# A neighbour pick on TensorE: three 16-bit parts in one product of 192 columns, added by the identity afterwards

## The chip, the cores and the metric

The kernel runs on one core of a Trainium2 chip. The metric is device time in microseconds (us) of one launch without profiling, the median of three runs. One more execution is recorded by the hardware profiler; durations of single instructions come from that one.

## The reference, cut to what matters

There are 16 graphs (called entries here) of 1024 nodes with 64 features. Four layers follow each other, each with a residual and a layer norm: a small perceptron on summed messages (layer 0), a normalised adjacency product (layer 1), and two layers that take three weighted quantiles over each node's neighbours, per feature, after a dilation that takes some neighbours away, and then a perceptron (layers 2 and 3).

```python
vals = jnp.where(valid[..., None], x[:, None, :, :], big)
sv = jnp.sort(vals, axis=2)
...
for tau, wt in zip(TAUS, QWEIGHTS):
    pos = jnp.clip(tau * (mf - 1.0), 0.0)
    lo = jnp.floor(pos).astype(jnp.int32)
    hi = jnp.ceil(pos).astype(jnp.int32)
    frac = (pos - lo.astype(x.dtype))[..., None]
    q = gather(lo) * (1.0 - frac) + gather(hi) * frac
    agg = agg + wt * q
```

The two quantile layers are called table layers 0 and 1 below. All features are 32-bit.

## The kernel before, in words

**Stages of an entry.** `features` computes the first two layers and marks the neighbours. `lists` does the dilation, counts each node's neighbours, ranks the nodes by that count and builds a permutation matrix `order` (16-bit ones and zeros). Sorted by count, the nodes lie in eight tiles of 128; a tile is sorted at a fixed width (10 to 33 slots, SIZES), so few slots are empty. `ordered` permutes the features into that order and writes them to a table in memory.

**Two ways to fetch neighbours.** For the seven tiles with few neighbours, `lists` makes index lists and GpSimd gathers rows from the table (`gather`, L372 and L373, one indirect DMA a slot, 2944 of them). For the last tile, whose nodes have most neighbours, TensorE picks the rows (`fill`, from L778): for slot i (a level, 1 to 32) a one-hot matrix `hot` of 128 x 1024 is made from `place` (the rank of each node in each list), and `pick` (L365 to L370) multiplies its eight blocks with the features. To be exact, 32-bit features are split into three 16-bit parts that sum to them (`split`, L402); so a pick is 8 blocks x 3 parts = 24 products of 64 columns, all accumulated in one 64-column place of PSUM. There are 32 levels x 16 entries x 2 table layers = 1024 picks.

**Around the pick.** Of four levels, three have their `hot` made by VectorE (`is_equal`, in `fill`) and one by ScalarE (L808 and L809). Six `hot` buffers rotate (HOTS). Four levels share half a PSUM bank (`pgs`, two halves); when four are done, `empty` copies them with two ScalarE copies of 64 partitions x 256 columns (L800), one for each half of the rows, into the sort buffers. The copies of a group are placed when the next group's second level has been issued. For levels of 20 and more, one further product (L817) puts a large number where a node has no such neighbour.

**Permuting.** `ordered` multiplies `order` with three small columns (count, row, mask: `own`, L670), then with the three parts of the features (L369, tile `ordered_x`, 8 tiles x 24 products), copies the sum out (L691), sends it to the table on SyncE's queue (L692), and hands it to `parted`, which splits it anew into three parts for the fill of table layer 0 (`x0p`). `parted` does the same for layer 1 (`x1p`).

**Order of the work.** All engines run a written order. The work goes in 16 rounds; in a round two entries of one table layer are sorted on VectorE by exchange networks (`exchange`; its instructions have L212), and between the exchange operations `Weave` issues steps of the other generators (features, lists, ordered, fill, weigh, finish). Its clock is an estimate of VectorE's time; each `yield n` puts the next step n us later on it. A fill yields 2.4 for a level. An instruction that waits holds back what stands behind it on its engine.

**Names.** `pgk` is the PSUM bank of the picks; `got` the sort buffers of the last tile; `got_s` the gathered ones; `rest` the remainder in a split; `x2s` the permuted features; `pk` the products that give the lists (L632, L640); `pr`, `pa`, `there_o` other products, used here for their rates (L530, L476, L705). `L850` weighs sorted slots, `L651` makes the codes from which VectorE finds the lists.

```python
    def pick(dst, hot, parts, first=True):
...
        for c in range(NT):
            for q in range(3):
                nc.tensor.matmul(dst, hot[:, c, :], parts[:, c, q, :], start=first and c + q == 0,
                                 stop=c == NT - 1 and q == 2)
```

Of the kernel before, what the change touches and what calls it, by code (L numbers as in the profile page):

```python
# [12 lines left out]
F32 = mybir.dt.float32  # L13
F16 = mybir.dt.float16
BF = mybir.dt.bfloat16
# [7 lines left out]
P = 128  # L23
# [10 lines left out]
TABLES = 6  # L34
HOTS = 6
ROOM = 60
# [181 lines left out]
def adj_resnorm_kernel(ctx: ExitStack, tc: tile.TileContext, x, adj_t, nodemask, w01, b01, w02, b02,  # L218
# [28 lines left out]
    ONSET = HALF - P  # L247
    steps = const.tile([P, ONSET + N], BF, name="steps")
    row_id = const.tile([P, NT], F32, name="row_id")
    nc.gpsimd.iota(row_id, pattern=[[P, NT]], base=0, channel_multiplier=1,  # L250
# [113 lines left out]

    def pick(dst, hot, parts, first=True):  # L365

        for c in range(NT):
            for q in range(3):
                nc.tensor.matmul(dst, hot[:, c, :], parts[:, c, q, :], start=first and c + q == 0,  # L369
                                 stop=c == NT - 1 and q == 2)  # L370

# [45 lines left out]
    def features(b, e):  # L417
# [71 lines left out]
        yield from settle(x2, y, "x")  # L489
        while b and entries[b - 1].xs[0] is None:  # L490
            yield 2
        parts = s.feat.tile([P, NT, 3, C], BF, name="x2p", bufs=1)
        yield from split(x2, parts, y)
        e.x2p = parts

    def lists(b, e, pace):
# [67 lines left out]
        first_ones = steps[:1, ONSET : ONSET + P]  # L564
        own = s.work.tile([P, NT, 3], F16, name="own", bufs=1)
        key = s.work.tile([P, 5, NT], F32, name="key_c", bufs=1)
# [22 lines left out]

        dve.tensor_scalar(own[:, :, 0], key[:, 4], 1.0, None, op0=ALU.add)  # L590
        dve.tensor_copy(own[:, :, 1], row_id)
        dve.tensor_copy(own[:, :, 2], mask)
        dve.scalar_tensor_tensor(key[:, 0], own[:, :, 0], float(N), row_id, op0=ALU.mult, op1=ALU.add)
        keys = s.psum.tile([P, N], F32, name="keys", tag="big", bufs=2)
# [3 lines left out]
        for t in range(NT):  # L598
# [3 lines left out]
            yield 1.4  # L602
        yield 6
        dve.tensor_scalar(key[:, 2], key[:, 1], float(N - 1), 0.5, op0=ALU.add, op1=ALU.mult)
# [15 lines left out]
        nc.scalar.activation(minus_at, pn[:1], AF.Copy, scale=-1.0 / N)  # L620
        weave.add(ordered(b, e, order, own), 1.5, pace)

        e.idx = s.feat.tile([P, LINKS[-1]], I32, name="idx", bufs=6)
        pks, codes, found = {}, {}, []
        for t in (*reversed(range(NT)), -1, -2, -3):
# [19 lines left out]
            if 0 <= done < NT:  # L645
                if done == NT - 1:
                    e.there = s.work.tile([P, NT, P], BF, name="there", bufs=1)
                    nc.scalar.activation(e.there.rearrange("p c n -> p (c n)"), pks[done], AF.Sign)
                else:
                    codes[done] = s.work.tile([P, N], F16, name="code", tag="dist", bufs=3)  # L650
                    nc.scalar.activation(codes[done], pks[done], AF.Relu, scale=float(N))  # L651
# [12 lines left out]

    def ordered(b, e, order, own):

        ps = s.psum.tile([P, NT, 3], F32, name="ps", tag="s", bufs=1)
        for t in range(NT):
            for c in range(NT):
                nc.tensor.matmul(ps[:, t, :], order[:, c, t * P : (t + 1) * P], own[:, c, :],  # L670
                                 start=c == 0, stop=c == NT - 1)
        yield 9
        sorted_own = s.work.tile([P, NT, 3], F32, name="sorted_own", bufs=1)
        nc.scalar.copy(sorted_own, ps)
        count = sorted_own[:, :, 0]
        while e.x2p is None:
            yield 2
        px = s.psum.tile([P, NT, C], F32, name="ordered_x", tag="s", bufs=1)
        for t in range(NT):
            pick(px[:, t, :], order[:, :, t * P : (t + 1) * P], e.x2p)  # L680
            if t % 2:
                yield 2.5
        e.out_rows = s.feat.tile([P, NT], I32, name="out_rows", bufs=8)
        dve.tensor_scalar(e.out_rows, sorted_own[:, :, 1], float(b * N), None, op0=ALU.add)
        e.mask = s.feat.tile([P, NT], F32, name="mask_s", bufs=8)
        dve.tensor_copy(e.mask, sorted_own[:, :, 2])
        yield 7
        while b >= 4 and entries[b - 4].xs[1] is None:
# [3 lines left out]
        nc.sync.dma_start(table[0][b % TABLES][:N, :].rearrange("(t p) c -> p t c", p=P), e.xs[0])  # L692
        weave.add(parted(b, e, 0))
        while e.there is None:
            yield 2

        yield 4
# [80 lines left out]
    def fill(k):  # L778

        while k and (k - 1, NS - 1) not in free:  # L780
            yield 1
        middle, most = SIZES[NS - 2], SIZES[NS - 1]
        ends = [s.lists.tile([P, size, C], F32, name="got", tag=f"got_{size}", bufs=1) for size in (middle, most)]
        tails[k] = ends
        layer, both = members(k)
        groups = 0
        for low, high in ((1, middle), (middle, most)):
            for m, b, e in both:
                while e.parts[layer] is None or e.xs[layer] is None or e.place is None or e.none is None:
                    yield 1  # L790
                at = [(rows, ends[plan - LISTED], SIZES[plan]) for rows, plan in zip((lower, upper), halves_of(b))]
                if low == 1:
                    for rows, got, _ in at:
                        nc.scalar.copy(got[rows, 0, :], e.xs[layer][rows, NT - 1, :])
                waiting = None

                def empty():
                    for rows, got, size in at:
                        if waiting[0] < size:
                            nc.scalar.copy(got[rows, waiting[0] : waiting[0] + 4, :], waiting[1][rows])  # L800

                for i in range(low, high):
                    if i % 4 == 1:
                        first, pg = i, pgs[groups % 2]
                        groups += 1

                        by_act = s.lists.tile([P, NT, P], BF, name="hot", bufs=HOTS)
                        nc.scalar.activation(by_act, e.place, AF.Abs, bias=minus_k[:, i + 2 : i + 3])  # L808
                        nc.scalar.activation(by_act, by_act, AF.Relu, bias=one_f, scale=-1.0)  # L809
                    if i % 4 == 3:  # L810
                        hot = by_act
                    else:
                        hot = s.lists.tile([P, NT, P], BF, name="hot", bufs=HOTS)
                        dve.tensor_scalar(hot, e.place, float(i), None, op0=ALU.is_equal)
                    whole = i < LEAST[NS - 2]
                    if not whole:
                        nc.tensor.matmul(pg[:, i - first, :], e.none,  # L817
                                         ident_b[: KW - 1, i - 1 : i].to_broadcast([KW - 1, C]), start=True, stop=False)
                    pick(pg[:, i - first, :], hot, e.parts[layer], whole)
                    yield 2.4  # L820
                    if i % 4 == 2 and waiting:
                        empty()
                    if i % 4 == 0:
                        waiting = first, pg
                yield 5
                empty()
                yield 0.5
                if high == most:
                    e.filled[layer] = True
            filled.add((k, low))  # L830
# [38 lines left out]
    def finish(b, e, layer, agg, spare=False):  # L869
# [37 lines left out]
        if layer == 0:  # L907
            nc.sync.dma_start(table[1][b % TABLES][:N, :].rearrange("(t p) c -> p t c", p=P), xn)
            e.xs[1] = xn
            weave.add(parted(b, e, 1))  # L910
            return
# [6 lines left out]

    def parted(b, e, layer):

        back = 2 if layer else 3
        while splitting or (b >= back and not entries[b - back].filled[layer]):
            yield 2
        splitting.add(b)
        parts = s.feat.tile([P, NT, 3, C], BF, name=f"x{layer}p", bufs=back)
        rest = s.feat.tile([P, NT, C], F32, name="rest", bufs=1)
        yield from split(e.xs[layer], parts, rest)
        splitting.remove(b)
        e.parts[layer] = parts

    class Weave:
# [34 lines left out]
        def finish(self, gen):  # L966
            while self.runs(gen):
                self.advance()

    entries = [SimpleNamespace(near=None, taken=False, packed=False, listed=False, there=None, placed=False, x2p=None, place=None, none=None,  # L970
                               wts=None, parts=[None, None], xs=[None, None], filled=[False, False], ends=None) for _ in range(B)]
# [135 lines left out]
    with ExitStack() as main:  # L1107
# [9 lines left out]
        picked = s.psum.tile([P, 8, C], F32, name="pgk", bufs=1)  # L1117
        pgs = [picked[:, :4, :], picked[:, 4:, :]]
        ring = s.lists.tile([P, 2, ROOM, C], F32, name="got_s")
# [294 lines left out]
```

## Time and profile before

| what | value |
|---|---|
| median of 3 runs | 5103.43 us (5102.24 to 5104.99) |
| the profiled execution | 6960.85 us |
| its span, first to last instruction | 6959.1 us |
| instructions in it | 112,002 |
| mean granted TensorE clock | 0.690 |
| VectorE busy | 4338.6 us |
| ScalarE busy | 2838.3 us |
| GpSimd busy | 3219.1 us |
| TensorE products, busy as modelled | 4047.0 us, 44,824 products |

The profiled execution is much longer than the timed ones, so shares of its span can't be carried over as they are. PE stands for TensorE's products, PEld for its weight loads (beside the products), DVE for VectorE, ACT for ScalarE, POOL for GpSimd, SP for SyncE. A row of a group has: line, engine, operation, tiles and shapes, count, busy time and mean ns of one, and the idle time of the engine just ahead with what ended it. Ends of products are modelled, so the rate of products is read from a run of them, not from one. In a table of stretches each engine has its busy time in that stretch and the number of its instructions; PEclk is the granted clock, as a share of full.

### The profile page before, as it was taken

Reading aid. Unit: us, or ns where it says so; the run is one execution under the profiler, and the core shown is the slowest. Engines: PE = TensorE matmul, PEld = TensorE weight load, DVE = VectorE, ACT = ScalarE, POOL = GpSimd, SP = SyncE. Lnnn points to the kernel's source line nnn. Section 1 sums busy time; section 2 is a strip of 40 time slices with the busy share of each in tenths; the row PEclk is TensorE's granted clock in tenths of the full one; section 3 lists DMA queues with packets and bytes.
Section 4 is the critical chain, followed back from the end, with each engine's and each line's share of the span. In section 5 each row is a group of like instructions: output and inputs, shape, how many; then the busy total and the mean of one; then the engine's idle time right before and its main releaser. Section 6 shows DMA issues by size and latency. Waiting matters only on the chain.

```text
span 6959.1 us, 112002 instructions
## 1 busy us (share of the span) xinstructions
PE 4047.0 (58%) x44824; PEld 2895.5 (42%) x44824; DVE 4338.6 (62%) x9272; ACT 2838.3 (41%) x6388; POOL 3219.1 (46%) x3168
## 2 busy tenths in 40 slices
PE   6757657386557665666666566665756563333243
PEld 5435435254334443444445344443534443223232
DVE  2446537577647668485665858566574767557575
ACT  4336335354344445344433535334353443223232
POOL 0342225625453545454454644455453645665551
PEclk8778777597668766767676667766667675555555
DMA  3111102111111111111111111111111100000100
GB/s 87 46 44 50 49 24 49 40 48 42 46 31 40 43 43 35 36 45 32 43 41 41 37 34 44 32 43 40 43 34 27 34 18 22 21 21 17 22 19 6
DMA packets 416527, 255.23 MB, mean 37 GB/s; under 512 B 104554, under 2 KB 366842, under 8 KB 415994
## 3 DMA queue, kind: packets, MB, share of 16 engines
q1 hardware_dynamic: 317690, 147.12, 7.7%
q0 software_dynamic: 98304, 100.86, 6.8%
q8 instruction: 352, 5.77, 0.3%
q14 instruction: 181, 1.48, 0.1%
HBM read 235.18 MB, written 12.59 MB: 36 GB/s over the span
## 4 chain that ended last, share of the span: by engine, by line
PE 34%; DVE 28%; issue 20%; another core or an unknown queue 8%; ACT 7%; POOL 1%; DMA 1%; DVEq 0%; ACTq 0%; POOLq 0%
PE pgk L369 11%; DVE other L212 11%; DVE got_s L212 7%; PE pk L640 6%; DVE got L212 5%; PE pa L476 4%; PE px L445 2%; PE ordered_x L369 2%; PE pr L530 1%; ACT got_s L850 1%; PE pk L632 1%; POOL got_s L373 1%; DVE hot L212 1%; PE pk L638 1%
## 5 line engine op out<-in xcount | busy, mean ns | idle before, releaser
L373 POOL DMA_INDIRECT got_s<-table,idx x2944 | 3075.3, 1045 | 3514.5 <-issue 784.3
L369 PEld LDWEIGHTS <-hot 128*128 128x128 bf16 x24576 | 1092.7, 112 | 1821.9 <-issue 1488.7
L369 PE MATMUL pgk<-x0p,hot 128*128 128x64 bf16 x12288 | 655.0, 212 | 694.6 <-issue 517.1
L369 PE MATMUL pgk<-x1p,hot 128*128 128x64 bf16 x12288 | 664.4, 216 | 646.5 <-issue 407.4
L800 ACT COPY got<-pgk 64x256 f32<-64x256 f32 x416 | 151.9, 365 | 1976.7 <-PE pgk L369 1352.4
L212 DVE TENSOR_SCALAR hot<-place 128x1024 bf16<-128x1024 f16 x768 | 332.0, 435 | 730.2 <-remote 518.2
L640 PE MATMUL pk<-near,order 128*128 128x512 fp8e4 x1792 | 495.9, 419 | 56.2 <-issue 54.0
L212 DVE TENSOR_TENSOR other<-got_s 128x512 f32<-128x512 f32 (+9 forms) x850 | 507.7, 608 | 29.8 <-ACT got_s L1035 15.3
L212 DVE TENSOR_TENSOR got_s<-got_s 128x512 f32<-128x512 f32 (+9 forms) x867 | 483.6, 560 | 18.4
L530 PE MATMUL pr<-steps,near 128*128 128x512 bf16 x1536 | 420.2, 436 | 96.8 <-ACT junk L536 72.5
L476 PE MATMUL pa<-x,adj_r 128*128 128x65 f32 x2048 | 359.7, 332 | 165.7 <-issue 156.9
L850 ACT ACTIVATE got_s<-got_s,wts 128x64 f32<-128x64 f32 x1568 | 393.8, 335 | 79.6 <-DVE got_s L212 70.7
L476 PEld LDWEIGHTS pa<-x,adj_r 128*128 128x128 f32 x2048 | 344.1, 251 | 177.5 <-issue 166.9
L212 DVE TENSOR_TENSOR got_s<-other 128x512 f32<-128x512 f32 (+9 forms) x731 | 401.2, 562 | 9.5 <-DVE other L212 1.5
L212 DVE TENSOR_TENSOR other<-other 128x384 f32<-128x384 f32 (+10 forms) x617 | 322.3, 522 | 17.1
L651 ACT ACTIVATE code<-pk 128x1024 f16<-128x1024 f32 x112 | 114.2, 1020 | 511.7 <-PE pk L640 344.5
L212 DVE MAX8 best<-code 128x8 f16<-128x1024 f16 x240 | 293.8, 1224 | 45.3 <-ACT code L651 32.3
L445 PE MATMUL px<-adj_r,x_s 128*64 128x128 f32 x2048 | 291.6, 299 | 47.4 <-issue 35.0
L640 PEld LDWEIGHTS <-order 128*128 128x128 bf16 x1792 | 167.3, 103 | 327.2 <-issue 197.4
L536 ACT ACTIVATE junk<-pr,nb_st 128x1024 f16<-128x1024 f32 x256 | 281.6, 1106 | 52.0 <-remote 21.8
L530 PEld LDWEIGHTS <-near 128*128 128x128 fp8e4 x1536 | 165.6, 110 | 327.9 <-issue 199.4
L809 ACT ACTIVATE hot<-hot,one_f 128x1024 bf16<-128x1024 bf16 x256 | 293.9, 1148 | 12.7 <-remote 4.4
(215 smaller groups left out, 7095.5 us busy)
## 6 DMA issues: line engine op xcount, KB each, us to landing
adj_r<-in_adj_dram SPq DMA_DIRECT2D x256, 512.0 KB
got_s<-table,idx POOLq DMA_INDIRECT x2944
x_s<-in_x_dram SPq DMA_DIRECT2D x16, 256.0 KB
table<-x2s SPq DMA_DIRECT2D x16, 256.0 KB
table<-x3s SPq DMA_DIRECT2D x16, 256.0 KB
out_dram<-agg,out_rows POOLq DMA_INDIRECT x128
table<-no_row SPq DMA_DIRECT2D x12, 0.2 KB
w01s<-in_L_gnn_W_dram SPq DMA_DIRECT2D x1, 32.0 KB
```

The source lines that it names most:

```text
L212: return call(*args, **kwargs)
L369: nc.tensor.matmul(dst, hot[:, c, :], parts[:, c, q, :], start=first and c + q == 0, stop=c == NT - 1 and q == 2)
L373: nc.gpsimd.indirect_dma_start(out=dst, out_offset=None, in_=tab, in_offset=bass.IndirectOffsetOnAxis(ap=rows, axis=0))
L445: nc.tensor.matmul(px[C:, q * P : (q + 1) * P], x_s[:, jt, :], adj[t][:, jt, :], start=jt == 0, stop=jt == NT - 1)
L476: nc.tensor.matmul(pa[:, q, :], adj[i][:, jt, :], x1[:, jt, :], start=jt == 0, stop=jt == NT - 1)
L530: nc.tensor.matmul(pr[:, h * HALF : (h + 1) * HALF], near[:, c, t * P : (t + 1) * P], steps[:, ONSET + h * HALF - c * P :][:, :HALF], star ...
L536: nc.scalar.activation(junk, prs[t - 1], AF.Sign, bias=lim[:, i, t - 1 : t], scale=-1.0, accum_out=cut_at[:, i, t - 1 : t])
L640: nc.tensor.matmul(cols, order[:, c, rows], left(c, slice(h * G, (h + 1) * G)), start=False, stop=c == NT - 1)
L651: nc.scalar.activation(codes[done], pks[done], AF.Relu, scale=float(N))
L800: nc.scalar.copy(got[rows, waiting[0] : waiting[0] + 4, :], waiting[1][rows])
L809: nc.scalar.activation(by_act, by_act, AF.Relu, bias=one_f, scale=-1.0)
L850: nc.scalar.activation(got[:, m, i, :], got[:, m, slot_id, :], AF.Copy, scale=e.wts[:, t, i : i + 1])
```

## The change

A pick becomes eight products of 192 columns: the three parts lie side by side, and the sum over the eight blocks is made for each part apart. ScalarE then copies the three sums (128 x 192, 32-bit in PSUM) to a 16-bit tile `brought`, and three products with the identity add them in PSUM. Each sum has one term that isn't zero, so the 16-bit copy loses nothing. Two places of 192 columns (`sides`), two of 64 (`pgs`) and two `brought` tiles rotate; all of PSUM's places are in the bank that `pgk` had. Copies into the sort buffers are made for two levels at a time, 64 x 128. The level's add is issued two levels after its pick, ScalarE's copy half a step before that add.

`ordered` works likewise: the split features and four small columns (count, two parts of the row number, mask) lie side by side in `moved` (196 columns), are permuted together in eight products a tile, two tiles at a time, and the copied parts serve the fill of table layer 0 as they are; three identity products of 512 columns give the 32-bit features. The second split for table layer 0 goes. Six `hot` buffers become five, and `there` becomes an 8-bit tile.

```diff
-HOTS = 6
+HOTS = 5
+OWN = 4
...
-    def pick(dst, hot, parts, first=True):
+    def pick(dst, hot, parts):
 
         for c in range(NT):
-            for q in range(3):
-                nc.tensor.matmul(dst, hot[:, c, :], parts[:, c, q, :], start=first and c + q == 0,
-                                 stop=c == NT - 1 and q == 2)
+            nc.tensor.matmul(dst, hot[:, c, :], parts[:, c, :, :], start=c == 0, stop=c == NT - 1)
+
+    def add_up(dst, parts, first=True):
+
+        for q in range(3):
+            nc.tensor.matmul(dst, ident_b, parts[:, q, :], start=first and q == 0, stop=q == 2)
...
-        yield 6
+        yield 9
...
+        while e.moved is None:
+            yield 1
+        moved = e.moved
+        dve.tensor_scalar(moved[:, :, 0], key[:, 4], 1.0, None, op0=ALU.add)
+        dve.tensor_copy(moved[:, :, 1:3], row_parts)
+        dve.tensor_copy(moved[:, :, 3], mask)
...
-                    e.there = s.work.tile([P, NT, P], BF, name="there", bufs=1)
+                    e.there = s.work.tile([P, NT, P], F8, name="there", bufs=1)
...
+        while not e.split or (b >= 3 and not entries[b - 3].filled[0]):
+            yield 1
+        sorted_own = s.work.tile([P, NT, OWN], F32, name="sorted_own", bufs=1)
+        parts = s.feat.tile([P, NT, 3, C], BF, name="x0p", bufs=3)
         count = sorted_own[:, :, 0]
-        while e.x2p is None:
-            yield 2
+        for g in range(0, NT, 2):
+            po = s.psum.tile([P, 2, OWN + 3 * C], F32, name="moved_o", tag="s", bufs=1)
+            for t in range(g, g + 2):
+                for c in range(NT):
+                    nc.tensor.matmul(po[:, t - g, :], order[:, c, t * P : (t + 1) * P], e.moved[:, c, :], start=c == 0,
+                                     stop=c == NT - 1)
+            yield 3.6
+            nc.scalar.copy(parts[:, g : g + 2], po[:, :, OWN:].rearrange("p t (q c) -> p t q c", c=C))
+            nc.scalar.copy(sorted_own[:, g : g + 2, :], po[:, :, :OWN])
+            yield 1.2
         px = s.psum.tile([P, NT, C], F32, name="ordered_x", tag="s", bufs=1)
-        for t in range(NT):
-            pick(px[:, t, :], order[:, :, t * P : (t + 1) * P], e.x2p)
-            if t % 2:
-                yield 2.5
+        for q in range(3):
+            nc.tensor.matmul(px, ident_b, parts[:, :, q, :], start=q == 0, stop=q == 2)
+        e.parts[0] = parts
...
-        weave.add(parted(b, e, 0))
...
-                    pick(pg[:, i - first, :], hot, e.parts[layer], whole)
-                    yield 2.4
-                    if i % 4 == 2 and waiting:
-                        empty()
-                    if i % 4 == 0:
-                        waiting = first, pg
...
+                for i in range(low, high + 3):
+                    if low <= i - 2 < high:
+                        at_i, sb = i - 2, brought[i % 2]
+                        whole = at_i < LEAST[NS - 2]
+                        pg = pgs[:, (at_i - low) % 2, :]
...
+                        add_up(pg, sb, whole)
+                    if i < high:
...
+                        pick(sides[i % 2], hot, e.parts[layer])
+                    yield 1.2
+                    if low <= i - 1 < high:
+                        nc.scalar.copy(brought[(i - 1) % 2], sides[(i - 1) % 2])
+                    if low <= i - 2 < high and (i - 2 - low) % 2:
+                        for rows, got, size in at:
+                            if i - 3 < size:
+                                nc.scalar.copy(got[rows, i - 3 : i - 1, :], pgs[rows])
+                    yield 1.2
...
-        pgs = [picked[:, :4, :], picked[:, 4:, :]]
+        sides = [picked[:, 3 * i : 3 * i + 3, :] for i in range(2)]
+        pgs = picked[:, 6:, :]
+        brought = [s.lists.tile([P, 3, C], BF, name=f"brought{i}") for i in range(2)]
```

The instruction lists of the two programs differ by: 24,576 weight loads of `hot` become 8192 and 6912 of `order` become 3840; 3120 products with the identity come in; on ScalarE 1024 copies of 128 x 192 and 832 of 64 x 128 come in, and 416 of 64 x 256 go. VectorE has 10,562 entries in both: 32 operations of 512 columns give way to small ones.

## The prediction

> **What bounds the kernel now.** I read the page first: engine totals, then the chain of work that ended last.
>
> ```profile
> PE 4047.0 (58%) x44824; PEld 2895.5 (42%) x44824; DVE 4338.6 (62%) x9272; ACT 2838.3 (41%) x6388; POOL 3219.1 (46%) x3168
> ...
> PE 34%; DVE 28%; issue 20%; another core or an unknown queue 8%; ACT 7%; POOL 1%; DMA 1%; DVEq 0%; ACTq 0%; POOLq 0%
> PE pgk L369 11%; DVE other L212 11%; DVE got_s L212 7%; PE pk L640 6%; DVE got L212 5%; PE pa L476 4%; PE px L445 2%; PE ordered_x L369 2%; PE pr L530 1%; ACT got_s L850 1%; PE pk L632 1%; POOL got_s L373 1%; DVE hot L212 1%; PE pk L638 1%
> ```
>
> It looks as if TensorE (PE) and its picks (L369) lead. But the profiled execution took 6960.85 us (span 6959.1, 1.75 around it) and the median is 5103.43: 1857 us are in the profiled execution only, or nearly. The chain says which: "issue" 19.5% and "unknown" 7.8% of 6959 are 1357 + 543 = 1900 us. The timeline shows what such a stretch is:
>
> ```profile
> 208.33 1.90 PE L476 MATMUL pa<-x,adj_r 128*128 128x65 f32 x16
> ...
> 242.52 0.29 PEld L476 LDWEIGHTS pa<-x,adj_r 128*128 128x128 f32 x1 [2.51 <-issue]
> 243.92 0.27 PE L476 MATMUL pa<-x,adj_r 128*128 128x65 f32 x1 [2.53 <-issue]
> 245.32 0.29 PEld L476 LDWEIGHTS pa<-x,adj_r 128*128 128x128 f32 x1 [2.51 <-issue]
> 246.72 0.27 PE L476 MATMUL pa<-x,adj_r 128*128 128x65 f32 x1 [2.53 <-issue]
> ```
>
> Sixteen products take 1.90 us; 35 us later one PE instruction starts every 1.40 us and waits for nothing shown. I take this as the price of recording 89,648 PE instructions, and look at stretches of 50 us in which issue and unknown are small:
>
> ```profile
> core 0: us, PE busy (x) PEld busy (x) DVE busy (x) ACT busy (x) POOL busy (x), PEclk, DMA share, GB/s
> 1400.00:1450.00 50.00, 49.17 (x639) 35.50 (x636) 44.77 (x78) 25.21 (x50) 0.00 (x0) 1.00 0.24 66
> 2150.00:2200.00 50.00, 42.94 (x615) 32.37 (x614) 47.42 (x110) 24.60 (x66) 15.17 (x16) 0.93 0.24 64
> 4300.00:4350.00 50.00, 30.35 (x334) 24.38 (x335) 48.30 (x94) 28.24 (x55) 24.82 (x23) 0.77 0.17 46
> 2600.00:2650.00 50.00, 29.60 (x155) 14.19 (x156) 47.81 (x114) 37.15 (x102) 22.88 (x22) 0.77 0.12 24
> 3450.00:3500.00 50.00, 20.16 (x133) 12.21 (x131) 48.51 (x102) 33.39 (x79) 34.80 (x30) 0.63 0.09 21
> ```
>
> The first three hold picks, the last two none. VectorE (DVE) is busy 44.8 to 48.5 of 50 us in all. And 4338.6 us of its work in 5103 is 85%; only 765 us are idle, much of it start and end. So the timed run is bound by DVE, and by PE only where picks meet other PE work (the first row).
>
> **What a pick costs.** The rate of PE is read from bursts on the chain:
>
> ```profile
> 313.90 0.70 PE pgk L369 x24
> ...
> 325.79 1.40 PE pgk L369 x48
> 327.19 2.59 PE pr L530 x12
> ```
>
> A load and a product of 64 columns: 0.70/24 = 29 ns. One of 512: 2.59/12 = 216. The 128-column products of L705 (32 in 1.79 us) take 56. That is 0.42 ns a column, with nothing for the weight load. The Trainium skill, "TensorE: Matmul & The Clock Gate", section "Back-to-back issue gap", gives N/2.4 + 2.5 ns and a floor near 25 ns: 29, 56 and 216, as here (its sustained 81 and 131 ns for 128 and 512 columns are not what this trace has). So 192 columns take an estimated 82 ns. The same page, section "Weight-path perf modes — Fast Weight Load (FWL) and DoubleRow", says a 16-bit load of 128 columns is sped up several times; the 29 ns agree. Loads are therefore no cost that sharing them could save.
>
> **The change part by part.** All against the profiled execution's rows; I carry the sum to the median, since the 1857 us between them are not in it.
>
> 1. *Picks* (32 levels x 16 entries x 2 layers = 1024). Removed: 24 pairs x 29 = 0.70 us. Added: 8 x 82 = 0.66 and three adds of 64 columns, 0.09: 0.75 us. +0.05 x 1024 = +51 us of PE at full clock, in proportion at half clock. PE ends a third of the chain: +17. Bounds: 0 (all beside DVE) and +51.
>
> 2. *ScalarE (ACT) copies.* Its rows:
>
> ```profile
> L800 ACT COPY got<-pgk 64x256 f32<-64x256 f32 x416 | 151.9, 365 | 1976.7 <-PE pgk L369 1352.4 <-remote 524.2 <-issue 37.2
> L452 ACT COPY node_in<-px 64x512 f32<-64x512 f32 x32 | 18.6, 580 | 50.9 <-remote 21.8 <-issue 16.1 <-PE px L445 12.6
> ```
>
> 0.84 ns a column, so 192 columns 0.31 us and 128 columns 0.26. Added: 1024 x 0.31 + 832 x 0.26 = 534; removed: 416 x 0.365 = 152. +382 us. ACT's "ScalarE: Activation LUTs", section "What ACT_TABLE_LOAD costs", has 186 ns + 0.833 a column, 346 for 192: same slope, 30 ns above these rows. Not shown before: a copy of 192 to bf16; I take 0.31 (bounds 0.23, overlapped, and 0.35). ACT ends 7% of the chain with 41% busy, 17% of its work: 382 x 0.17 = +65. Bounds: 0, since ACT was idle 2265 us of 5103, and +150, where each late copy holds up what is queued behind it (weighing L850, code L651), for which DVE waits.
>
> 3. *Ordering* (16 times). Removed: 192 x 29 + 64 x 25 = 7.2 us of PE; added 64 x 84 (196 columns) + 3 x 216 = 6.0. -19 in all; a third: -6. ACT: 64 copies of 384 (0.47) and 64 of 8 (0.15) for 48 casts of 0.6 and 16 small copies: +8, nothing on the path. The table's write on SP's queue and POOL's gathers behind it now follow four rounds of products and copies through one bank, some 4 x 0.6 us of ACT later; from the third pair on this lies beside the round before, for the first entries it is exposed: +2, in the rounding. The 8-bit "there" (L648), the two iotas and the list's new wait for the split rows cost nothing that I can name: the same products and copies, and rows that are split a layer earlier than they are used.
>
> 4. *The second split of layer 0 goes.*
>
> ```profile
> L212 DVE TENSOR_TENSOR rest<-x2s,x0p 128x512 f32<-128x512 f32 x16 | 11.0, 688 | 49.5 <-ACT x0p L405 34.2 <-issue 15.3
> L212 DVE TENSOR_TENSOR rest<-rest,x0p 128x512 f32<-128x512 f32 x16 | 11.0, 687 | 40.1 <-issue 31.7 <-ACT x0p L409 8.2
> ```
>
> -22 us of DVE; 32 small operations (about 0.17 each) come in: +5. Before them DVE sat 90 us; 47 are "issue". Of 42 for ACT I take 20. Sum -37; bounds -107 and -17.
>
> 5. *Slack.* Hot tiles 6 to 5, and the pick's room from eight levels to two: PE's add waits for ACT's copy of a level issued only half a step before, and queued behind that add are the later picks and all else in PE's order. Who waits: DVE, at the next hot tile, its queue with it.
>
> ```profile
> DVE hot L212 <- PE pgk L369: 200.7, 49, 19.9
> ```
>
> In the first clean stretch that wait was 4.0 of 50 us, in the other two none. Fills take some 170 of each round's 290 us, 2700 us in all; a third more of a wait of at most 8% is +70, at least 0. I take +20. New small wait: ordering holds for a layer-0 fill three entries back; it comes a round before the gathers need it, so nothing.
>
> Sum: +17 + 65 - 6 - 37 + 20 = +59. Made against the profiled execution without its stalls: 6960.85 - 1900 = 5061, within 1% of the median. Forecast 5103 + 59 = 5162, say **5160**.
>
> **Rivals.** (a) *ACT in lockstep with PE*: copies at 1024 places where ACT waits for the pick just issued, against 208. For: L800 alone waited 1977 us. Against: ACT has 2265 - 390 = 1875 us free. It decides when a level's wait passes 1875/1024 = 1.8 us; at 2.0 us ACT is the bound: 2838 + 390 + 2048 = 5276. (b) *Fewer instructions help the timed run too; faster.* DVE's work at 95% busy is 4339/0.95 = 4567; start idle is some 200 us (233 in the first 350). 336 us of 5103 stay unexplained. If they are PE stalls of the kind in the timeline and go with PE's instructions (89,648 to 56,976, -36%), that is -121: 5162 - 121 = 5041, and 4945 where parts 2 and 5 are hidden as well. Against: 1900 us of stall match the whole excess of the profiled execution. It decides from 59/0.36 = 164 us of such stalls on. (c) *Nothing moves*: copies are hidden, slack is enough, part 4 is eaten: 5103 within 0.2%.
>
> **Numbers.** Forecast (slower, 5115 to 5230) 0.44; (a) 0.11; (b) 0.34, most of it from 4945 to 5090; (c) 0.11. Two in ten outside: low 4960 (nearly all of (b)), high 5290 (just past (a)'s). A difference below 0.2% can't be told from none here. Slower 0.55, same 0.11, faster 0.34.
>
> **What would show it.** Pick: 8 products in about 0.7 us on the chain, PE's busy time for them not smaller per level. ACT busy up by 300 to 400 us; DVE down by some 17. The profiled span should fall far more than the median: stalls 1900 x 0.64 = 1208, so about 6370, with 80,840 instructions. Lockstep would show as ACT's "brought" copies waiting for picks over 1.8 us each. I am wrong if clean stretches show DVE busy no less, yet the median falls over 100 us: then the stalls were in the timed run; or if products of 192 columns take clearly less than 82 ns.

## Result, and the profile after

The changed kernel takes 5480.36 us (median of 4 runs, 5478.82 to 5482.86); the kernel before 5103.78 beside it. The ratio is 1.0738, with a 95% interval of 1.072 to 1.0757: slower by 377 us, not by the 57 forecast, and above the range. Several chips were used: on some the kernel before has medians of 5103 to 5105 us, on others of 6986 to 7001, so every ratio below is within one chip. Differences in us between runs of the first kind can be across its chips, which agree within 2 us in the medians of the kernel before. Both medians here are of the first kind; the profile of before, with its 6960 us and 27% of its chain spent waiting for nothing shown, was probably taken on the second (the record doesn't name its chip).

The page of the changed kernel, engine totals and chain:

```profile
span 5478.8 us, 81153 instructions
PE 3723.2 (68%) x28385; PEld 2701.2 (49%) x28488; DVE 4330.0 (79%) x9272; ACT 3181.8 (58%) x7898; POOL 3319.1 (61%) x3170
...
PE 35%; DVE 33%; ACT 20%; issue 4%; POOL 3%; DMA 3%; ACTq 0%; DVEq 0%; POOLq 0%
```

The span is that of the other runs, and "issue" is 4% of the chain instead of 20%. DVE has about the same work as before (4330 against 4338.6) but is idle 1149 us. For a comparison of idle time the profile of before is of no use, being so much longer; the nearest on the first kind of chip is the kernel with the new ordering and the old picks (e15 below):

```profile
span 5068.0 us, 106032 instructions
PE 3474.6 (69%) x41800; PEld 2592.5 (51%) x41800; DVE 4314.6 (85%) x9272; ACT 2842.5 (56%) x6452; POOL 3338.3 (66%) x3170
```

There DVE is idle 753 us. The spans differ by 411 us, and 395 of these are idle DVE. Busy time per 500 us shows that the loss is found in all three stretches looked at, not in one place. First the changed kernel, then e15:

```profile
1000.00:1500.00 500.00, 348.51 (x2673) 250.78 (x2685) 415.78 (x875) 293.74 (x716) 301.55 (x282) 0.79 0.24 56
2000.00:2500.00 500.00, 354.73 (x2742) 256.15 (x2751) 439.37 (x935) 319.40 (x814) 340.38 (x313) 0.77 0.22 49
3000.00:3500.00 500.00, 345.36 (x2621) 251.51 (x2633) 440.81 (x954) 323.06 (x795) 332.66 (x306) 0.76 0.22 50
```

```profile
1000.00:1500.00 500.00, 373.60 (x4450) 274.95 (x4450) 457.35 (x942) 313.89 (x699) 339.60 (x313) 0.83 0.25 59
2000.00:2500.00 500.00, 393.27 (x4944) 295.48 (x4941) 462.62 (x982) 305.59 (x708) 379.39 (x349) 0.83 0.25 59
3000.00:3500.00 500.00, 361.71 (x4420) 269.23 (x4420) 468.35 (x1001) 313.33 (x706) 360.82 (x329) 0.83 0.24 57
```

The columns after the window's length are busy PE, PEld, DVE, ACT and POOL. DVE does 416 to 441 us of work in a window instead of 457 to 468. PE and POOL do less than there too, and ACT about the same (936 us in the three windows, against 933). So no other engine has become full; they wait for one another.

The groups that answer to L800 and to the split's remainder:

```profile
L831 ACT CAST brought<-pgk 128x192 bf16<-128x192 f32 x1024 | 323.5, 316 | 1201.8 <-PE pgk L373 1157.5 <-PE pgk L378 38.9 <-issue 0.5
L378 PE MATMUL pgk<-brought,ident_b 128*128 128x64 bf16 x3072 | 296.1, 212 | 429.6 <-ACT brought L831 245.2 <-ACT got L835 184.2
L835 ACT COPY got<-pgk 64x128 f32<-64x128 f32 x832 | 216.1, 260 | 45.4 <-PE pgk L378 40.2
```

```profile
L213 DVE TENSOR_TENSOR rest<-x3s,x1p x16: 683/685/693, 932.8 to 5127.9; 128x512 f32<-128x512 f32 x16
```

Sizes are as forecast: 0.316 us a copy (0.31), 0.26 a sum's copy, and only layer 1 is still split in `parted`. What the forecast didn't have: ACT sat 1158 us ahead of the copies, waiting for picks, and PE 429 us ahead of the additions, waiting for ACT. DVE's wait at the hot tiles:

```profile
DVE hot L213 <- PE pgk L373: 274.7, 95, 9.9
```

(total, times, longest). It was 50.6 in e15, which has six hot tiles. In e3 below, with five of them and the old fill, it was 115.5, so a part of the rise may belong to the missing tile. Added up by cause over DVE's waits, PE went from 179 to 443 us, ACT from 241 to 406, DMA from 151 to 116: +394, the difference in idle time (395) but for rounding.

The timeline shows how it goes, here 12 us of a fill of layer 1:

```profile
2010.16 0.82 PE L373 MATMUL pgk<-x1p,hot 128*128 128x192 bf16 x8
...
2011.02 0.32 ACT L831 CAST brought<-pgk 128x192 bf16<-128x192 f32 x1 [1.06 <-PE pgk L373]
...
2011.39 0.25 PE L378 MATMUL pgk<-brought,ident_b 128*128 128x64 bf16 x3 [0.41 <-ACT brought L831]
...
2013.38 1.15 ACT L821 ACTIVATE hot<-place,minus_k 128x1024 bf16<-128x1024 f16 x1
...
2013.49 0.82 PE L373 MATMUL pgk<-x1p,hot 128*128 128x192 bf16 x8
...
2014.56 1.15 ACT L822 ACTIVATE hot<-hot,one_f 128x1024 bf16<-128x1024 bf16 x1
...
2015.74 0.32 ACT L831 CAST brought<-pgk 128x192 bf16<-128x192 f32 x1
...
2016.11 0.25 PE L378 MATMUL pgk<-brought,ident_b 128*128 128x64 bf16 x3 [1.79 <-ACT brought L831]
...
2021.03 1.47 PE L373 MATMUL pgk<-x1p,hot 128*128 128x192 bf16 x8
...
2022.53 0.32 ACT L831 CAST brought<-pgk 128x192 bf16<-128x192 f32 x1 [1.69 <-PE pgk L373]
```

By the code, the copy behind pick i takes the side of pick i - 1, which was done long before. Yet at 2011.02 and 2022.53 it starts 0.04 and 0.03 us after the *newest* pick ends (2010.98, 2022.50), with ACT idle for over a microsecond ahead of it. So the two sides are no two buffers: the copy waits for the last product into `pgk`, whatever its place. The built program says the same: 1020 of the 1024 copies wait for the newest product into `pgk` that was issued ahead of them (for the other four, ACT had made that wait before), and where an addition waits for a copy out of `pgk`, it is the newest one. And the next addition waits for that copy, if need be behind two 1.15 us activations for a hot tile, which stand ahead of it on ACT (1.79 us). Each level sends PE to ACT and back.

### The profile page after: what moved, and what is told of

The parts are those of the page before. It is cut to its first block, busy times and chain, and to the rows that moved or that the text cites. A ratio compares the mean times of both kernels' runs of the same rounds, so it can differ in the third digit from the quotient of the medians.

```text
span 5478.8 us, 81153 instructions
## 1 busy us (share of the span) xinstructions
PE 3723.2 (68%) x28385; PEld 2701.2 (49%) x28488; DVE 4330.0 (79%) x9272; ACT 3181.8 (58%) x7898; POOL 3319.1 (61%) x3170
## 4 chain that ended last, share of the span: by engine, by line
PE 35%; DVE 33%; ACT 20%; issue 4%; POOL 3%; DMA 3%; ACTq 0%; DVEq 0%; POOLq 0%
DVE other L213 12%; PE pgk L373 9%; DVE got_s L213 8%; PE pk L651 6%; DVE got L213 6%; PE pa L484 4%; ACT brought L831 3%; ACT hot L822 2%; ACT got_s L859 2%; PE px L453 2%; DMA got_s<-table,idx 2%; ACT hot L821 2%; POOL got_s L381 2%; PE pgk L378 2%; ACT got L835 2%
## 5 line engine op out<-in xcount | busy, mean ns | idle before, releaser
L381 POOL DMA_INDIRECT got_s<-table,idx x2944 | 3175.6, 1079 | 1966.7 <-issue 631.7
L831 ACT CAST brought<-pgk 128x192 bf16<-128x192 f32 x1024 | 323.5, 316 | 1201.8 <-PE pgk L373 1157.5
L373 PEld LDWEIGHTS <-hot 128*128 128x128 bf16 x8192 | 851.5, 119 | 325.7 <-DVE hot L213 278.9
L373 PE MATMUL pgk<-x1p,hot 128*128 128x192 bf16 x4096 | 587.0, 306 | 221.2 <-DVE hot L213 205.4
L378 PEld LDWEIGHTS <-ident_b 128*128 128x128 bf16 x3072 | 214.5, 108 | 826.7 <-issue 798.7
L378 PE MATMUL pgk<-brought,ident_b 128*128 128x64 bf16 x3072 | 296.1, 212 | 429.6 <-ACT brought L831 245.2
L373 PE MATMUL pgk<-x0p,hot 128*128 128x192 bf16 x4096 | 551.0, 293 | 48.7 <-DVE hot L213 42.2
L213 DVE TENSOR_TENSOR got_s<-got_s 128x128 f32<-128x128 f32 (+10 forms) x867 | 484.1, 562 | 44.1 <-ACT got_s L859 26.0
L651 PE MATMUL pk<-near,order 128*128 128x512 fp8e4 x1792 | 434.9, 387 | 0.0
L821 ACT ACTIVATE hot<-place,minus_k 128x1024 bf16<-128x1024 f16 x256 | 293.3, 1146 | 7.3 <-DVE place L213 3.7
```

What stands on the lines that cost most here:

```text
L213: return call(*args, **kwargs)
L373: nc.tensor.matmul(dst, hot[:, c, :], parts[:, c, :, :], start=c == 0, stop=c == NT - 1)
L378: nc.tensor.matmul(dst, ident_b, parts[:, q, :], start=first and q == 0, stop=q == 2)
L381: nc.gpsimd.indirect_dma_start(out=dst, out_offset=None, in_=tab, in_offset=bass.IndirectOffsetOnAxis(ap=rows, axis=0))
L651: nc.tensor.matmul(cols, order[:, c, rows], left(c, slice(h * G, (h + 1) * G)), start=False, stop=c == NT - 1)
L831: nc.scalar.copy(brought[(i - 1) % 2], sides[(i - 1) % 2])
```

## Experiments

Theory (lockstep): what costs is each place in ACT's order at which it must stop for the newest pick, and PE's stop for ACT after it. First rival: ScalarE's added work. Second: the wider products and additions on TensorE, or the fifth hot tile gone.

**The parts alone.** e1 takes the changed kernel's ordering, and the picks, six hot tiles and copies by fours of before; e2 the opposite; e3 is the kernel before with `HOTS = 5`; e4 the changed kernel without the copies.

```diff
 # e1, against the changed kernel
-HOTS = 5
+HOTS = 6
...
-                        pick(sides[i % 2], hot, e.parts[layer])
+                    pick(pg[:, i - first, :], hot, e.parts[layer], whole)
...
 # e2, against the kernel before: the other way round
 # e3, against the kernel before
-HOTS = 6
+HOTS = 5
 # e4, against the changed kernel
-                    if low <= i - 1 < high:
-                        nc.scalar.copy(brought[(i - 1) % 2], sides[(i - 1) % 2])
...
+        for still in brought:
+            nc.vector.memset(still, 1.0)
```

> The new ordering (features and small columns permuted side by side, no second split for table layer 0) with the picks, the six hot tiles and the group copies of before. If the loss comes from the hand-over of each pick between TensorE and ScalarE (lockstep), this is at or a little below the kernel before: 5040 to 5110 us. If it comes from the ordering, whose wait for an earlier fill makes the gathers late, it is 5250 us or more. By the forecast's part 4 alone it gains some 40 us.

> The new picks with five hot tiles, the ordering and its second split as before. Lockstep: most of the loss stays, 5420 to 5560 us. If the ordering is to blame, under 5300 us.

> The kernel before with five hot tiles in place of six, nothing else. Lockstep: a small cost, 5105 to 5150 us. If the missing hot tile makes VectorE wait for TensorE, 5250 us or more.

> The changed kernel without ScalarE's copies of the three sums (the adds take a constant tile, so the picked features are left out of the last tile's values). 1024 copies of 0.316 us and both hand-overs of each are gone. Lockstep, or ScalarE's added work: 5000 to 5200 us. If the ordering, the hot tiles or the products themselves are to blame: over 5380 us.

Beside 5105.1 us of before: e1 5066.93 (ratio 0.9924, 0.9907 to 0.994), e2 5565.94 (1.0897, 1.0878 to 1.0915), e3 5112.04 (1.0012, 1.0005 to 1.0019), e4 5179.02 (1.0133, 1.0109 to 1.0157). The ordering gains 38 us, the fill loses 5480 - 5067 = 413 on top of it, and leaving out the copies gives 301 of these back. With the old ordering the fill loses 461 (e2; 6 us above the range expected, the other three lie in theirs). A hot tile less costs 7 us in the kernel before; in the changed kernel, a sixth one was not tried. From e4 to the changed kernel, PE's waits for ACT's copies out of `pgk` rise from 286 to 672 us, and ACT's waits ahead of these copies from 991 to 1237. But e4 doesn't yet tell the copies' work from their waits.

**The copies' work kept, the waits cut.** In e5, e9 and e13, one and the same kernel, ACT makes the same 1024 copies at the same places, of a tile in SBUF into a tile nobody reads.

```diff
-                        nc.scalar.copy(brought[(i - 1) % 2], sides[(i - 1) % 2])
+                        nc.scalar.copy(unread, e.xs[layer][:, :3, :])
...
+        unread = s.lists.tile([P, 3, C], BF, name="unread")
+        for still in brought:
+            nc.vector.memset(still, 1.0)
```

All three stood on chips of the second kind, the last with the changed kernel beside it (e14).

> The changed kernel, where ScalarE still makes 1024 copies of 128x192 values at the same places in its order, but from a tile in SBUF into a tile that nobody reads; the additions by the identity take two constant tiles. So the picked values never reach the result; the work of all engines stays, and only the two hand-overs (TensorE to ScalarE and back) are gone. Lockstep theory (the changed kernel loses its time because the copy waits for a pick and the next pick waits for the copy): near the kernel without the copies, 5180 to 5240 us. ScalarE-work theory (324 us more of busy ScalarE hold up its other work, whoever waits for whom): ScalarE's work is as before, so 5400 us or more. Half and half would stand near 5320.

> The kernel with ScalarE's 1024 copies kept but cut from the picks, as before (the picked values don't reach the result), for a second set of runs, since the first stood on a chip where the kernel before takes 6986 us. Where that kernel takes 5105 us: lockstep theory 5180 to 5260 us, ScalarE-work theory 5400 us or more, both by half near 5320. Where it takes 6986 us again: 6740 as before, and only the comparison with the next three counts.

> The kernel with ScalarE's 1024 copies kept but cut from the picks (the picked values don't reach the result), a third time, because the two earlier sets stood on chips where the kernel before takes about 7000 us. Where that kernel takes 5105 us: lockstep theory 5180 to 5260 us; ScalarE-work theory 5400 us or more; half and half near 5320. Where it takes 7000 us again: some 6750, and the comparison with the changed kernel beside it counts alone.

> The changed kernel itself, beside the last one on the same chip. Where the kernel before takes 5105 us: 5480 as in the first measurement. Where it takes 7000 us: the loss of 377 us need not be the same there, since the kernel before spends some 1900 us in stretches in which engines wait for nothing shown; with a third fewer TensorE instructions the changed kernel may spend less in them. If those stretches go with the instructions: 7000 + 377 - 0.36 x 1900 = 6690 us, faster than before. If they don't: about 7370.

e5 6739.45 us, e9 6754.82, e13 6720.64; before 6986.05, 7000.55 and 6986.62 beside them. e14, the changed kernel, 7016.54 (7013.92 to 7057.91), ratio 1.0063 (1.0033 to 1.0092). So cutting the waits takes 296 us off on the same chip (e13's runs spread from 6691 to 6767), with all of the work in place; its copies are even longer:

```profile
L831 ACT CAST unread<-x2s 128x192 bf16<-128x192 f32 x512 | 177.0, 346 | 5.5 <-ACT unread L831 0.5
L831 ACT CAST unread<-x3s 128x192 bf16<-128x192 f32 x512 | 176.4, 344 | 4.5
```

That is as much as leaving the copies out altogether gave on the other kind of chip (301). So the waits, not the work, carry the copies' cost on the second kind. That the work itself costs next to nothing on the first kind too holds only as far as the two kinds may be set side by side; no run tests it on one chip. Two hand-overs are cut here at once, from PE to ACT and back, and which of them costs more is not separated.

**More room, later copies.** Without the third part (products of 128 columns) the bank has room for more.

```diff
 # e6 and e11, against the changed kernel
-            nc.tensor.matmul(dst, hot[:, c, :], parts[:, c, :, :], start=c == 0, stop=c == NT - 1)
+            nc.tensor.matmul(dst, hot[:, c, :], parts[:, c, :2, :], start=c == 0, stop=c == NT - 1)
...
-        for q in range(3):
+        for q in range(2):
...
 # e7, against e6 (and three tiles "brought")
-        sides = [picked[:, 2 * i : 2 * i + 2, :] for i in range(2)]
+        sides = [picked[:, 2 * i : 2 * i + 2, :] for i in range(3)]
...
-                        at_i, sb = i - 2, brought[i % 2]
+                        at_i, sb = i - 3, brought[i % 3]
...
 # e8, against e7
-                    if low <= i - 1 < high:
-                        nc.scalar.copy(brought[(i - 1) % 3], sides[(i - 1) % 3])
+                    if low <= i - 2 < high:
+                        nc.scalar.copy(brought[(i - 2) % 3], sides[(i - 2) % 3])
 # e10 against e9, e12 against e11, e18 against e4 (e10 and e18 with one side)
-        pgs = picked[:, 6:, :]
+        pgs = [picked[:, 4 + 2 * i : 6 + 2 * i, :] for i in range(2)]
...
-                        pg = pgs[:, (at_i - low) % 2, :]
+                        pg = pgs[(at_i - low) // 2 % 2][:, (at_i - low) % 2, :]
...
```

> The changed kernel without the third 16-bit part in the picks, so products of 128 columns and two additions a level; two sides, as in the changed kernel. It leaves the smallest part out of the picked features. It is the partner of the next two, which need the room in the bank. TensorE has some 8 x 26 + 29 = 0.24 us less a level (about 245 us in all), ScalarE's copy is 0.06 us shorter (about 58 in all). Both theories: between 5250 and 5420 us.

> As the last one, without the third part, but with three sides in the bank and three copies in SBUF, and the additions of a level three places after its pick: a pick now waits for the copy of three levels before, not of two. Instructions and their sizes are the same as with two sides. Lockstep theory: the wait of TensorE for ScalarE (179 us in a kernel with the old picks, 672 in the changed one) falls by half or more, and the time by 100 us or more against two sides. ScalarE-work or TensorE-work theory: within 20 us of two sides.

> As the last one, without the third part and with three sides, but ScalarE's copy of a level one place later as well (after the next pick but one is in the order), so that ScalarE doesn't stand waiting for the newest pick. TensorE's slack is that of two sides again, ScalarE's is a level longer. Lockstep theory, if it is ScalarE's standing (1158 us of waits in the changed kernel) that holds up its other work: ScalarE's wait for picks falls to a third, and the time to within 20 us of the three sides with the early copy, or below; if it is TensorE's waiting that counts: near two sides. ScalarE-work theory: the same as two sides within 20 us.

> As the last one (copies kept, but of a tile that no pick writes; the picked values don't reach the result), and the sums go into two pairs of places by turns instead of one, so that the sum of a pair no longer waits for ScalarE's copies of the pair just before. All work of the changed kernel is in it, neither loop is tight. Lockstep theory, with the second loop as the cause of what the kernel without copies kept (112 us over the kernel with the new ordering alone): 60 to 110 us less than with one pair, and TensorE's wait for the got copies, 273 us in the changed kernel, under 100. Work theory: within 20 us of the last one.

> The changed kernel without the third part, two sides and one pair of places, again, as the partner of the next one. Where the kernel before takes 5105 us: 5250 to 5420 by both theories.

> As the last one, without the third part, but with two pairs of places for the sums by turns (there is room in the bank). Instructions and sizes are the same; only the second loop, sums and got copies, is looser. The earlier trial with three sides moved nothing, and its TensorE went on waiting some 600 us for the got copies. Lockstep theory: TensorE's wait for got falls by half or more and the time by 50 to 120 us against one pair. Work theory: within 20 us of one pair.

> The kernel without ScalarE's copies of the picks (the additions take a constant tile, so the picked values don't reach the result), and with two pairs of places for the sums instead of one. With one pair it took 5179 where the kernel before takes 5105, with 286 us of TensorE waiting for the got copies. Lockstep theory: 50 to 110 us less than that with two pairs (on a chip where the kernel before takes 7000 us: below the 6720 to 6755 of the kernels with cut copies). Work theory: within 20 us.

On chips of the second kind e6 took 6884.53 (ratio 0.9818), e7 6898.61 (0.9856), e8 6854.99 (0.978; runs of 6832 to 6892 against e6's 6853 to 6909 and e7's 6887 to 6918), e11 6864.99, e12 6881.28, e10 6750.65 beside e9's 6754.82; on the first kind e18 took 5176.24 beside e4's 5179.02. What I had expected of the looser rings failed in e7, e10, e12 and e18. e8's time, 44 us under e7's, was allowed for, but the sign that I had named for it did not show: ACT's waits for products ahead of the copies of picks were 866 us in both. For the pairs of places the reason is plain: in the built programs of e9 and e10, e11 and e12, e4 and e18 every wait is the same, instruction for instruction and value for value. More places inside one tile loosen no wait, because a wait is for the tile (or for its bank: no kernel here tells these apart). These trials are repeats of one program, and no evidence for or against lockstep. With a third side (e7, e8) the copies and additions shift by a level in the code, but in the built programs 1021 and 1020 of the 1024 copies still wait for the newest product into `pgk`. So these two did not loosen the wait that they were meant to loosen, and don't test lockstep either.

**The rest of the loss: the sums' copies by twos.** e16 is the changed kernel with the picks of before, straight into the sum's place: no copies of picks, no additions, but five hot tiles and the copies into `got` by twos, right behind the second pick. e17 has four pairs of places.

```diff
 # e16, against the changed kernel
-                        pick(sides[i % 2], hot, e.parts[layer])
+                    pick(pg, hot, e.parts[layer], whole)
...
-                                nc.scalar.copy(got[rows, i - 3 : i - 1, :], pgs[rows])
+                                nc.scalar.copy(got[rows, i - 1 : i + 1, :], pair[rows])
...
 # e17, against e16
-        pgs = [picked[:, 2 * i : 2 * i + 2, :] for i in range(1)]
+        pgs = [picked[:, 2 * i : 2 * i + 2, :] for i in range(4)]
```

> The kernel with the new ordering alone, again, as the partner of the next two on their chip. Where the kernel before takes 5105 us: 5067. Where it takes 7000 us: DVE has 17 us less to do and the rest is as in the kernel before; both theories 6940 to 7000.

> The changed kernel with the picks of before (24 products of 64 columns, straight into the place of the sum), so without the 1024 copies and without the additions by the identity; but with its five hot tiles and its got copies of two levels (832 of 64x128) through one pair of places, where each pick after a pair waits for the copies just issued. This is the second loop alone. Lockstep theory with the second loop as the cause of the other 112 us: 5130 to 5200 where the kernel before takes 5105 us, and in any case 60 to 130 us above the kernel with the new ordering alone. If that loop is harmless (then the added products and wider columns are the rest): within 25 us of it.

> As the last one, but with four pairs of places by turns, the whole bank, as much room as in the kernel before. Copies and picks are the same in number and size; only the second loop is loose. Lockstep theory: within 25 us of the kernel with the new ordering alone. Work theory (twice as many got copies, 64 us more of ScalarE): the same as the last one.

Beside 5104.78 of before: e15 5062.78 (0.9915, 0.9899 to 0.9932), e16 5226.42 (1.024, 1.0223 to 1.0257), e17 5240.21 (1.0257, 1.0239 to 1.0274). e17's waits are again those of e16 to the last value, so it tests nothing. It took 14 us more all the same; differences of that size between two kernels are not to be relied on. e16 loses 164 us to e15, with the same picks; I had expected 60 to 130. ACT's longest waits, in e15 and then in e16:

```profile
ACT got L811 <- PE pgk L374: 653.3, 168, 24.9
```

```profile
ACT got L827 <- PE pgk L374: 960.9, 343, 19.1
```

The places at which ACT stops for the newest pick are twice as many: 416 against 208. Its work grew by 72 us only (2842.5 to 2914.7). But e16 differs in more than the number of stops: each copy comes right behind its own pair's second pick, the steps in the written order are finer, and a hot tile is gone. That the stops make the 164 us is argued, not shown.

**The account.** 208 places: 5063 us (e15). 416: 5226 with the old picks (e16), 5179 with the new ones (e4). 1024: 5480 (the changed kernel). From e4 to the changed kernel that is 301/608 = 0.50 us a place; from e15 to e16 (164 - 7 for the hot tile)/208 = 0.75, if all of it is put down to the stops. Step by step from the kernel before to the changed one: ordering -42, sums by twos and the hot tile +164, wide products and additions in place of narrow ones -47, copies +301; together +376. These are differences along one row of kernels, so that they add up to the measured 377 is no test of the account.

## Why the prediction was wrong

The sign was right, and so were parts 3 and 4; the size was off by 320 us. Two terms were short, by 236 (copies) and 144 us (slack, by the row of kernels above); picks were 64 too high.

1. *Picks*, forecast +17 (0 to +51). The durations held: in the changed kernel's trace the starts of such products lie 82 to 84 ns apart where they come fastest (140 to 160 in other stretches); eight take 0.82 us on the timeline from the first start to the last end. The Trainium skill, "TensorE: Matmul & The Clock Gate", section "Back-to-back issue gap", gives N/2.4 + 2.5 for N columns, so an estimated 82.5 ns for 192; the trace agrees. PE's busy time rose by 67 us (3474.6 in e15, 3541.8 in e18). But the time fell by 47 from e16 to e4. The additions come two levels after their pick, and there are 13,312 fewer products; which of these helps is not separated.

2. *ScalarE's copies*, forecast +65 with bounds of 0 and +150; measured +301. **This is the step that failed.** The added work was sized rightly (323.5 + 216.1 - 151.8 = 388 us in the rows against 382), but I charged it by ACT's share of the chain, as if it were work that lies on the path one time in six, and that share did not stay: ACT ends 8% of the chain in e15 and 20% in the changed kernel. With the work kept and only the waits cut, 296 us went away (e13 against e14). Each copy is a place at which ACT stops for PE, PE then for ACT, and DVE for both. The loss goes with these stops, not with the microseconds of copying; that every stop has the same price is not shown (0.50 and 0.75 us above).

3. and 4. *Ordering and the second split*, forecast -6 - 37 = -43; measured -38 (e1) and -42 (e15). DVE's work fell by 20 us (4334.1 in e3, 4314.6 in e15), against 17 forecast.

5. *Slack*, forecast +20 with bounds of 0 and +70; measured +164. The hot tile was a small part of it, going by its 7 us in the kernel before (e3). I had named the added wait and who stands behind it, but taken it as a third more of a small wait; the 416 stops behind the second level of each pair were in no term of the sum. How much of the 164 they make is open.

*Rivals.* (a) had the mechanism, ACT waiting for the pick just issued, and a wrong threshold: I let it decide only when ACT is full, from 1.8 us a level on. It lost 301 us at a mean wait of 1157.5/1024 = 1.13 us with ACT 58% busy. So no engine had to be full for it. (b) and the stalls: I read 1857 us of the profile as the price of recording. That was wrong. The profile of e3 has this:

```profile
span 5112.0 us, 111972 instructions
```

That is as many instructions as in the profile of before but 30. The run that it shows took 5113.82 us, the other 19 of that kernel 5107.66 to 5115.36. On the second kind of chip, all runs of the kernel before take about 7000 us. The forecast of a span of 6370 was void with it: 5478.8 on one kind, 7015.3 on the other. On the second kind a gain of (b)'s sort is seen: the excess over the first kind falls from 1882 us to 1536, which nearly pays for the loss (ratio 1.0063). But it isn't in proportion to PE's instructions, which fell by 36%, and whether it comes from them isn't shown; e14's 7016.54 lies between the 6690 and the 7370 expected. On the chips of the medians such stretches were hardly there to be saved ("issue" is 4% of the changed kernel's chain and 5% of e15's). A slip in (b) besides: with parts 2 and 5 hidden as well, 5041 - 65 - 20 is 4956, not 4945.

Not tried: sides and sums as tiles of their own, in this bank or in others, so that a wait could be for one side. The bank was one tile in every kernel here. Nor was the changed kernel run with six hot tiles. Open too are what the stretches on the second kind of chip are, and how much of e16's loss comes from its finer steps in the written order.

The version that beats both kernels is e1, the new ordering with the old fill, though by less than 1%: 0.9924 (0.9907 to 0.994) of the kernel before, and 0.9915 again in e15.

## What to carry to other kernels

When a change sends a value from one engine to another and back at each step, count the places at which an engine in a written order must stop for another's newest instruction, and price those places (0.50 us here by the copies, up to 0.75 by the sums), not the busy time of what is added there. Look in the built program at whether slots of a ring are separate objects for the waits: one, two and four pairs of places in one tile had the same waits here. Then set a profile's unexplained stalls against a second profile before putting them down to recording.

## What the hardware showed beside that

- The same program took 5102 to 5110 us in every run on some chips (e1's and e15's among them) and 6965 to 7037 in every run on three others (those of e5, e9 and e13). On the latter the chain holds long shares of waiting for nothing shown, in the changed kernel too (e14); why is open:

```profile
PE 31%; DVE 20%; ACT 20%; another core or an unknown queue 18%; issue 8%; POOL 1%; DMA 1%; ACTq 0%; DVEq 0%; POOLq 0%
```

- ScalarE's cast of 128x192 took 316 ns from PSUM and 344 to 346 from SBUF. The Trainium skill, "ScalarE: Activation LUTs", section "What ACT_TABLE_LOAD costs", has 186 ns + 0.833 a column for an activation with immediate scale and bias, so an estimated 346: right for the SBUF source, 30 ns too much for PSUM. The kind of chip isn't the reason: e14 has 317 ns from PSUM on the chip where e13 has 344 to 346.
